# A decoder layer's query and key projections: one Newton operation moved to GpSimd, and a rotation that adds up in its PSUM bank

## The chip, the cores and the metric

The kernel runs on one core of one Trainium2 chip. The metric is the device time of one execution in microseconds (us); lower is better. The core has five engines with a queue of instructions each, worked through in order: TensorE (PE, matrix products), VectorE (DVE, elementwise), ScalarE (ACT, functions of one input), GpSimd (POOL, reductions across partitions and general work) and SyncE (SP, which only issues transfers here). Data lies in SBUF, and products land in PSUM, in eight banks.

## The reference

One decoder layer on 8 sequences of 100 tokens, width 1024, in float32: a retention block (8 heads), a cross-attention block with a context of 722 tokens (16 query heads, 4 key/value heads of 128), and a gated feed-forward block with 4096 hidden units, each followed by a residual sum and a layer norm. The change is in the second block's projections, of which the reference says:

```python
q = rms_norm(q, q_norm_w)          # x * rsqrt(mean(x*x, -1) + eps) * w, over a head's 128 numbers
k = rms_norm(k, k_norm_w)
...
q = q * cos + rotate_half(q) * sin
k = k * cos + rotate_half(k) * sin
k_full = jnp.concatenate([k_ctx, k], axis=1)
```

## The kernel before

Activations lie transposed: 128 features on the partitions, tokens along the row. The 800 tokens are worked on in two halves of N = 400. To keep float32 accuracy at the speed of the shorter format, each operand is split in a high and a low part, and each product is three matmuls (lines 91, 94 and 95): high by high, high by low, low by high. A projection of 1024 features to one head (`proj`) is 8 x 3 = 24 matmuls into one PSUM bank. The banks are shared out as three accumulators "a", four banks "s" and one "v".

The stages follow one another: the retention block, its output projection and norm, the second projections (the loop around lines 670 to 687), the attention over the context, its output projection and norm, the feed-forward block, and the last norm.

In the second projections a loop runs over 4 key/value heads, over pairs of weights (four for the first head), the two halves and the weights: four q heads, one k and one v per key/value head. So there are 40 groups of q or k and 8 of v; between them stand 4 halves of early context keys (`context_keys`, whose squares are summed on POOL too). For each q or k group:

- PE makes the projection in a bank "a".
- ACT squares it (L673), and POOL sums the squares over the partitions, to all of them (`all_red`, L141). `sq` and `ss` have two buffers each.
- `rope` rotates: ACT copies the two halves of the partitions, swapped, to a bank "s" (L149, L150); DVE multiplies the projection by the cosine to SBUF (L151), the swapped copy by the sine in its bank (L152), and adds them to SBUF (L153).
- `inv_root` makes the inverse root of sum + eps: ACT's logarithm with eps as bias (L128), exponential (L131) and square (L133) give a first guess r and its square, and one Newton step on DVE refines it: q = (sum + eps) * r*r (L134), then (q - 3) * r (L136). With `at=` a second bank "s" holds r and the result.
- DVE scales the rotated values (L678), ACT and DVE split them in high and low parts (L68, L69), and SP stores them to memory (L682), from where the attention loads them.

The order of each engine's instructions is not written out: the program is built with a scheduler that simulates the engines, and it reorders the work of the loop, within its dependences and its buffers. Some loads and norms are pinned. On POOL, the all-reduce and the elementwise operations belong to different libraries of code, and the build puts a library load ahead of an instruction whose library may not be resident. In this kernel there are two: one at the start, before an affine select that makes the identity matrix, and one before the first all-reduce.

Of the kernel before, what the change touches and what calls it, by code (L numbers as in the profile page):

```python
# [8 lines left out]
F32 = mybir.dt.float32  # L9
FR = mybir.dt.float32r  # L10
AF = mybir.ActivationFunctionType
ALU = mybir.AluOpType
# [4 lines left out]
P = 128  # L17
B, T, D = 8, 100, 1024
NB = 4
N = NB * T  # L20
# [20 lines left out]
def decoder_layer(ctx, tc, xT, cT, w1, wo1, w2, wo2, wc, w3, wd, gw, qw, kw, trig, dec, mask, out):  # L41
    nc = tc.nc

    def sbuf(name, bufs, side=None):
        return tc.tile_pool(name=name, bufs=bufs, side=side, reuse_waits="tile")
# [8 lines left out]
    def bank(tag):  # L54
        return ps.tile([P, 512], F32, tag=tag, name=tag, bufs=banks[tag])

    def f32(ap):
        return ap.bitcast(F32)

    def bt(ap):  # L60
        return ap.rearrange("p (b t) -> p b t", b=NB)
# [5 lines left out]
    def split2(hi, lo, src):  # L67
        nc.scalar.copy(hi, src)  # L68
        nc.vector.tensor_tensor(lo, src, f32(hi), ALU.subtract)  # L69

    def load_w(src, w=None, pinned=False):
        st = wp.tile([P, KT * P], F32, tag="wst", name="wst", bufs=3)
        if w is None:
            w = wp.tile([P, 2, KT * P], FR, tag="w", name="w", bufs=4)
        nc.sync.dma_start(out=st, in_=src)
        if pinned:
            tc.keep_in_program_order(nc.scalar.copy(w[:, 0], st))
            nc.vector.tensor_tensor(w[:, 1], st, f32(w[:, 0]), ALU.subtract)  # L78
        else:
            split(w, st)  # L80
        return w
# [6 lines left out]
    pin = tc.keep_in_program_order  # L88
# [25 lines left out]
    def proj(w, z, n=N, tag="a", todo=None):  # L114
        acc = bank(tag)[:, :n]
        for k in range(KT):
            pinned = between(todo, k)
            t = z[k // QT]
            mmw(acc, w, k, t[:, 0, k % QT, :n], t[:, 1, k % QT, :n], k == 0, k == KT - 1, pinned)
        return acc  # L120
# [1 line left out]
    def ln_exp():  # L122
        tc.keep_in_program_order(nc.scalar.preload_act_table_set(LN_EXP))

    def inv_root(pool, ss, eps, n=N, pin=False, at=None):

        r = pool.tile([P, n], F32, tag="r0", name="r0") if at is None else at
        ln = nc.scalar.activation(r, ss, AF.Ln, bias=eps)  # L128
        if pin:
            tc.keep_in_program_order(ln)  # L130
        nc.scalar.activation(r, r, AF.Exp, scale=-0.5)  # L131
        q = pool.tile([P, n], F32, tag="r1", name="r1")
        nc.scalar.activation(q, r, AF.Square)  # L133
        nc.vector.scalar_tensor_tensor(q, ss, eps, q, ALU.add, ALU.mult)  # L134
        out = q if at is None else at
        nc.vector.scalar_tensor_tensor(out, q, 3.0, r, ALU.subtract, ALU.mult)  # L136
        return out

    def all_red(pool, x, tag, op=RED.add):
        y = pool.tile([P, N], F32, tag=tag, name=tag)  # L140
        nc.gpsimd.partition_all_reduce(y, x, P, op)  # L141
        return y

    def rope(pool, acc, cosw, sinw, tag="t1", op=ALU.add, swapped=None):

        t1 = pool.tile([P, N], F32, tag=tag, name=tag)
        t2 = pool.tile([P, N], F32, tag="t2", name="t2") if swapped is None else swapped
        h = P // 2
        nc.scalar.copy(t2[0:h], acc[h:P])  # L149
        nc.scalar.copy(t2[h:P], acc[0:h])  # L150
        nc.vector.tensor_tensor(bt(t1), bt(acc), cosw[:, None, :].to_broadcast([P, NB, T]), ALU.mult)  # L151
        nc.vector.tensor_tensor(bt(t2), bt(t2), sinw[:, None, :].to_broadcast([P, NB, T]), ALU.mult)  # L152
        nc.vector.tensor_tensor(t1, t1, t2, op)  # L153
        return t1

    def tokens_first(pool, acc, copied=True):

        vt = acc
        if copied:
            vt = pool.tile([P, N], F32, tag="vt", name="vt", bufs=1)  # L160
            nc.scalar.copy(vt, acc)
        tr = bank("s")
        for b in range(NB):
            nc.tensor.transpose(tr[0:T, b * P:(b + 1) * P], vt[:, b * T:(b + 1) * T], ident)  # L164
        return tr[0:T]
# [30 lines left out]
    def const(v, name):  # L196
        t = cp.tile([P, 1], F32, name=name)
        nc.vector.memset(t, v)
        return t
# [3 lines left out]
    eps_k = const(128e-6, "eps_k")  # L203
# [238 lines left out]
    with sbuf("l1", 2) as p:  # L442
# [49 lines left out]
        qk, v, oo, ss = {}, {}, {}, {}  # L492
# [114 lines left out]
    def load_context(b):  # L607

        cz.clear()
        for hf in range(2):  # L610
            n = SN[hf]
            z = [big([P, 2, QT, SH]) for _ in range(2)]
            for k in range(0, KT, 2):
                cs = wp.tile([P, KT * P], F32, tag="wst", name="cs", bufs=3)
                cs = cs[:, :2 * n].rearrange("p (k n) -> p k n", k=2)
                nc.sync.dma_start(out=cs, in_=cT[b, :, k:k + 2, hf * SH:hf * SH + n])
                split(z[k // QT][:, :, k % QT:k % QT + 2, :n], cs)
            cz.append(z)

    def context_keys(kv):  # L620

        kall = ka.tile([P, 2, SC + T], FR, tag="kall", name="kall")
        wk = load_ws(2 * kv)
        sq = ka.tile([P, SC], F32, tag="ksq", name="ksq", bufs=1)
        ss = ka.tile([P, 6 * P], F32, tag="kss", name="kss", bufs=1)
        row = dr.tile([6, P], F32, tag="row", name="row", bufs=2)
        nc.gpsimd.memset(ss[:, SC:], 1.0)

        def step(hf):
            n, at = SN[hf], slice(hf * SH, hf * SH + SN[hf])  # L630
            acc = proj(wk, cz[hf], n)
            nc.scalar.activation(sq[:, at], acc, AF.Square)  # L632
            nc.gpsimd.partition_all_reduce(ss[:, at], sq[:, at], P, RED.add)  # L633
            nc.scalar.activation(kall[:, 0, at], acc, AF.Copy, scale=kws)
            nc.vector.scalar_tensor_tensor(kall[:, 1, at], acc, kws, f32(kall[:, 0, at]), ALU.mult, ALU.subtract)
            if hf:
                nc.sync.dma_start(out=row.rearrange("c p -> (c p)")[None, :], in_=ss[0:1])
        return step, (kall, row)
# [12 lines left out]
    with sbuf("l2", 2) as p:  # L651
        for kv in range(NKV):
            for i0, i1 in ((0, 4), (4, 6)) if kv == 0 else ((0, 2), (2, 4), (4, 6)):
                if (kv, i0) == (0, 4):
                    load_context(0)
                ws = [load_w(w2[kv, i]) for i in range(i0, i1)]
                if (kv, i0) in ((1, 2), (2, 2)):
                    step, kept = context_keys(kv - 1)
                    early.append(kept)
                if (kv, i0) in ((1, 2), (2, 0), (2, 2), (3, 0)):  # L660
                    step(i0 == 0)
                for half in range(2):
                    bs = slice(half * NB, (half + 1) * NB)
                    for i in range(i0, i1):
                        acc = proj(ws[i - i0], z1[half])
                        if i == 5:
                            tr = tokens_first(p, acc).rearrange("p (b d) -> p b d", b=NB)
                            vs = p.tile([T, NB, 2, P], FR, tag="vs", name="vs", bufs=1)
                            split2(vs[:, :, 0], vs[:, :, 1], tr)
                            nc.sync.dma_start(out=f32(vd[kv, :, bs]), in_=f32(vs))  # L670
                            continue
                        sq = p.tile([P, N], F32, tag="sq", name="sq")
                        nc.scalar.activation(sq, acc, AF.Square)  # L673
                        ss = all_red(p, sq, "ss")
                        tb = tq if i < 4 else tk
                        t = rope(p, acc, tb[:, 0], tb[:, 1], swapped=bank("s")[:, :N])
                        r = inv_root(p, ss, eps_k, at=bank("s")[:, :N])
                        nc.vector.scalar_tensor_tensor(  # L678
                            t, t, -0.5 if i < 4 else -0.5 * math.sqrt(P), r, ALU.mult, ALU.mult)
                        d = p.tile([P, NB, 2, T], FR, tag="d", name="d", bufs=3)  # L680
                        split2(d[:, :, 0], d[:, :, 1], bt(t))
                        nc.sync.dma_start(out=f32(qd[kv, i, :, bs] if i < 4 else kd[kv, :, bs]), in_=f32(d))  # L682
# [5 lines left out]
    with sbuf("cx", 2) as p, sbuf("c1", 1) as p1:  # L688
# [6 lines left out]
        for b in range(B):  # L695
            if b > 0:
                load_context(b)
            for kv in range(NKV):
# [10 lines left out]
                q = p.tile([P, 4, 2, T], FR, tag="q", name="q")  # L709
# [13 lines left out]
                r0 = p.tile([P, 6], F32, tag="rr0", name="rr0")  # L723
# [9 lines left out]
                s = p1.tile([P, NC, N], F32, tag="s", name="s")  # L733
# [5 lines left out]
                for j, c in enumerate(ORDER):  # L739
                    rows, n, t0 = (R6, N6, T6) if c == 6 else (P, N, 0)  # L740
# [35 lines left out]
                for j in (1, 0, 2, 3, 4, 5, 6):  # L776
                    c = ORDER[j]
                    n = N6 if c == 6 else N
# [4 lines left out]
                r = p.tile([P, N], F32, bufs=1, tag="r0", name="r0")  # L783
# [74 lines left out]
    for half in range(2):  # L858
        for i in range(2):
            ag, au = (proj(w, z2[half], tag=acc_tag()) for w in ws[i])  # L860
            t = temp()
# [221 lines left out]
    with sbuf("ln3", 1, "right") as lnp:  # L1083
        ws, todo = [], {}
        for half in range(2):
            y = rows(half)
            s1 = lnp.tile([P, N], F32, tag="s1", name="s1", bufs=2)
            for m in range(KT if half == 0 else KT - 2):
# [5 lines left out]
                acc = proj(ws[m], z3[half], tag=acc_tag(), todo=todo.pop(m, None))  # L1094
# [92 lines left out]
```

## Time and profile before

Median of three executions: 2505.04 us (2503.92 to 2506.51). The profiled execution took 2506.91 us, of which its span, the first to the last record, is 2505.1 us; the granted TensorE clock was 0.995 in the mean.

| | busy us | share of the span |
|---|---|---|
| TensorE (PE) | 2459.8 | 98% |
| VectorE (DVE) | 1952.1 | 78% |
| ScalarE (ACT) | 1340.7 | 54% |
| GpSimd (POOL) | 464.9 | 19% |
| the second projections, first to last square (L673) | | 612.0 to 836.1 us |

How to read the profile's lines: a group's line has the source line, engine, operation, output <- inputs, shapes and count, then busy time and the mean of one in ns, then the idle time of the engine just before these instructions and what ended it. A line of the timeline has the start and the duration in us, and in brackets the idle time before it and its releaser. "issue" is idle time in which the engine waited for nothing that the profile shows. A "q" behind an engine's name is its sequencer, which also issues transfers. In the stretches, each engine has its busy time and the number of instructions; PEclk is the clock that was granted to TensorE. Times of matmuls overlap, since they are pipelined.

### The profile page before, as it was taken

How to read it: one execution, taken by the hardware profiler on the slowest of the kernel's cores; microseconds unless marked ns; L12 is line 12 of the kernel's file. 1: busy time of each engine (PE TensorE's matmuls, PEld its weight loads, DVE VectorE, ACT ScalarE, POOL GpSimd, SP SyncE). 2: the span in 40 equal slices, each digit the busy share in tenths (PEclk: the TensorE clock that was granted, in tenths of full speed). 3: DMA queues.
4: the chain of work that ended last, by engine and by line, in shares of the span. 5: the costliest groups of instructions: out<-in, count | busy, mean ns of one | idle time of the engine just before them, and what ended most of it. 6: DMA issues, size and time to landing. Idle time of an engine off the chain costs nothing.

```text
span 2505.1 us, 37227 instructions
## 1 busy us (share of the span) xinstructions
PE 2459.8 (98%) x14068; PEld 2438.5 (97%) x14068; DVE 1952.1 (78%) x3101; ACT 1340.7 (54%) x2260; POOL 464.9 (19%) x234
## 2 busy tenths in 40 slices
PE   9999999997999999999999999999999999999997
PEld 9999999997899999999999999999999999999997
DVE  7678877567877688988989999866987777666756
ACT  6667676334767556566565666533544444432221
POOL 0111111001445343433434434100000000000000
PEclk9999999998999999999999999999999999999999
DMA  7333445774543654554554563675455444389731
GB/s 241 111 111 128 136 143 181 242 271 128 170 148 131 215 172 150 167 175 143 166 186 134 170 199 110 215 246 162 141 176 197 165 168 168 128 282 329 273 102 53
DMA packets 224451, 433.98 MB, mean 173 GB/s; under 512 B 47338, under 2 KB 168042, under 8 KB 211854
## 3 DMA queue, kind: packets, MB, share of 16 engines
q1 hardware_dynamic: 222542, 426.87, 50.7%
q0 software_dynamic: 1152, 4.19, 1.0%
q8 instruction: 111, 1.82, 0.3%
q14 instruction: 70, 0.57, 0.1%
q10 hardware_dynamic: 576, 0.52, 0.1%
HBM read 322.18 MB, written 109.35 MB: 172 GB/s over the span
## 4 chain that ended last, share of the span: by engine, by line
PE 91%; DVE 4%; DMA 3%; ACT 1%; issue 1%; POOL 0%; SPq 0%; DVEq 0%; ACTq 0%; POOLq 0%
PE a L95 19%; PE a L91 19%; PE a L94 19%; PE s L95 9%; PE s L94 9%; PE s L91 9%; PE v L95 1%; PE v L91 1%; PE v L94 1%; PE s L518 1%; PE s L716 1%; DMA cs<-in_cT 1%; DMA wst<-in_w 1%; PE s L164 1%; DVE big L69 0%
## 5 line engine op out<-in xcount | busy, mean ns | idle before, releaser
L91 PE MATMUL a<-big,w 128*128 128x400 f32 (+2 forms) x1808 | 609.0, 338 | 4.9 <-ACT big L68 1.8
L94 PE MATMUL a<-big,w 128*128 128x400 f32 (+2 forms) x1808 | 609.0, 337 | 0.7 <-DVE big L69 0.6
L95 PE MATMUL a<-big,w 128*128 128x400 f32 (+2 forms) x1808 | 608.1, 337 | 0.9 <-DVE w L78 0.9
L68 ACT CAST w<-wst 128x1024 fp32r<-128x1024 f32 (+1 forms) x229 | 237.5, 1039 | 389.5 <-PE s L95 134.6
L69 DVE TENSOR_TENSOR w<-wst,w 128x1024 fp32r<-128x1024 f32 (+1 forms) x229 | 280.5, 1226 | 137.8 <-ACT w L68 136.4
L91 PEld LDWEIGHTS a<-big,w 128*128 128x128 f32 x1808 | 339.6, 188 | 7.1 <-ACT big L68 2.3
L94 PEld LDWEIGHTS a<-big,w 128*128 128x128 f32 x1808 | 340.2, 188 | 2.5 <-DVE big L69 1.5
L95 PEld LDWEIGHTS a<-big,w 128*128 128x128 f32 x1808 | 340.2, 188 | 2.0 <-DVE w L78 1.3
L91 PE MATMUL a<-z,w 128*128 128x400 f32 x680 | 234.8, 345 | 21.2 <-DVE t L151 18.6
L95 PE MATMUL a<-z,w 128*128 128x400 f32 x680 | 235.8, 347 | 0.0
L94 PE MATMUL a<-z,w 128*128 128x400 f32 x680 | 235.7, 347 | 0.0
L91 PE MATMUL s<-big,w 128*128 128x400 f32 x664 | 230.5, 347 | 0.1
L95 PE MATMUL s<-big,w 128*128 128x400 f32 x664 | 229.0, 346 | 0.4 <-DVE w L69 0.4
L94 PE MATMUL s<-big,w 128*128 128x400 f32 x664 | 229.1, 345 | 0.0
L141 POOL PARTITION_ALL_REDUCE ss<-sq x56 | 150.9, 2697 | 328.2 <-DMA zd<-y 171.2
L633 POOL PARTITION_ALL_REDUCE kss<-ksq x64 | 167.2, 2613 | 130.3 <-ACT ksq L632 127.6
L91 PEld LDWEIGHTS a<-z,w 128*128 128x128 f32 x680 | 128.3, 189 | 23.0 <-DVE t L151 16.0
L750 ACT ACTIVATE s<-s,rk 128x400 f32<-128x400 f32 x160 | 87.8, 591 | 92.9 <-DVE sm L770 68.1
L95 PEld LDWEIGHTS a<-z,w 128*128 128x128 f32 x680 | 129.0, 190 | 0.3
L94 PEld LDWEIGHTS a<-z,w 128*128 128x128 f32 x680 | 128.2, 189 | 0.2
L91 PEld LDWEIGHTS s<-big,w 128*128 128x128 f32 x664 | 124.6, 188 | 1.4 <-ACT w L68 0.4
L95 PEld LDWEIGHTS s<-big,w 128*128 128x128 f32 x664 | 125.1, 188 | 0.7 <-DVE w L69 0.7
(361 smaller groups left out, 5439.3 us busy)
## 6 DMA issues: line engine op xcount, KB each, us to landing
wst<-in_w SPq DMA_DIRECT2D x135, 512.0 KB
w<-wcd SPq DMA_DIRECT2D x64, 1024.0 KB
wst<-in_wo SPq DMA_DIRECT2D x64, 512.0 KB
hd<-h SPq DMA_DIRECT2D x12, 1400.0 KB
wst<-in_wd SPq DMA_DIRECT2D x64, 256.0 KB
big<-o1d SPq DMA_DIRECT2D x16, 800.0 KB
qd<-d SPq DMA_DIRECT2D x32, 400.0 KB
q<-qd SPq DMA_DIRECT2D x32, 400.0 KB
```

Of the source, the lines that this page charges most:

```text
L68: nc.scalar.copy(hi, src)
L69: nc.vector.tensor_tensor(lo, src, f32(hi), ALU.subtract)
L91: i = nc.tensor.matmul(acc, lh, rh, start=start, stop=False, skip_group_check=chain)
L94: nc.tensor.matmul(acc, lh, rl, start=False, stop=False, skip_group_check=chain)
L95: nc.tensor.matmul(acc, ll, rh, start=False, stop=stop, skip_group_check=chain)
L141: nc.gpsimd.partition_all_reduce(y, x, P, op)
L164: nc.tensor.transpose(tr[0:T, b * P:(b + 1) * P], vt[:, b * T:(b + 1) * T], ident)
L518: nc.tensor.matmul(bt(o)[:, b], vv[:, b * P:(b + 1) * P], pf[:, b], start=True, stop=True)
L633: nc.gpsimd.partition_all_reduce(ss[:, at], sq[:, at], P, RED.add)
L716: nc.tensor.transpose(tr[0:rows, (c - c0) * P:(c - c0 + 1) * P], vt[:, c * P:c * P + rows], ident)
L750: nc.scalar.activation(sc, sp, AF.Copy, scale=rk[:, c:c + 1])
```

## The change

For the q and k groups of the second projections alone:

- The rotation's sum (L153 before) goes to the bank of the swapped copy in place of SBUF, and the scaling works on it there; the split reads the bank. `t1` is free after the sum.
- The first guess and its square lie in SBUF, so that one bank "s" serves a group in place of two.
- The first operation of the Newton step, (sum + eps) * r*r, leaves DVE. POOL adds eps to the sum in place, ACT's logarithm follows that addition and has no bias, and POOL multiplies by the square of the guess.
- The second operation, q - 3 times the guess, becomes q - 3 times the rotated values, and the scaling multiplies by the guess.

Other callers of `inv_root` and `rope` do what they did.

```diff
+    def root_guess(pool, ss, eps, n=N, pin=False):
+        r = pool.tile([P, n], F32, tag="r0", name="r0")
+        ln = nc.scalar.activation(r, ss, AF.Ln) if eps is None else nc.scalar.activation(r, ss, AF.Ln, bias=eps)
+        if pin:
+            tc.keep_in_program_order(ln)
         nc.scalar.activation(r, r, AF.Exp, scale=-0.5)
         q = pool.tile([P, n], F32, tag="r1", name="r1")
         nc.scalar.activation(q, r, AF.Square)
+        return r, q
+
+    def inv_root(pool, ss, eps, n=N, pin=False):
+        r, q = root_guess(pool, ss, eps, n, pin)
         nc.vector.scalar_tensor_tensor(q, ss, eps, q, ALU.add, ALU.mult)
-        out = q if at is None else at
-        nc.vector.scalar_tensor_tensor(out, q, 3.0, r, ALU.subtract, ALU.mult)
-        return out
+        nc.vector.scalar_tensor_tensor(q, q, 3.0, r, ALU.subtract, ALU.mult)
+        return q
...
-    def rope(pool, acc, cosw, sinw, tag="t1", op=ALU.add, swapped=None):
+    def rope(pool, acc, cosw, sinw, tag="t1", op=ALU.add, swapped=None, out=None):
...
-        nc.vector.tensor_tensor(t1, t1, t2, op)
+        nc.vector.tensor_tensor(t1 if out is None else out, t1, t2, op)
...
                         ss = all_red(p, sq, "ss")
                         tb = tq if i < 4 else tk
-                        t = rope(p, acc, tb[:, 0], tb[:, 1], swapped=bank("s")[:, :N])
-                        r = inv_root(p, ss, eps_k, at=bank("s")[:, :N])
+                        t = bank("s")[:, :N]
+                        rope(p, acc, tb[:, 0], tb[:, 1], swapped=t, out=t)
+
+                        nc.gpsimd.tensor_scalar_add(ss, ss, eps_k)
+                        r, q = root_guess(p, ss, None)
+                        nc.gpsimd.tensor_tensor(q, ss, q, ALU.mult)
+                        nc.vector.scalar_tensor_tensor(t, q, 3.0, t, ALU.subtract, ALU.mult)
                         nc.vector.scalar_tensor_tensor(
                             t, t, -0.5 if i < 4 else -0.5 * math.sqrt(P), r, ALU.mult, ALU.mult)
```

More of the change, by code (lines that the diff above doesn't have):

```diff
@@ L123, in ln_exp @@
         tc.keep_in_program_order(nc.scalar.preload_act_table_set(LN_EXP))
-    def inv_root(pool, ss, eps, n=N, pin=False, at=None):
-        r = pool.tile([P, n], F32, tag="r0", name="r0") if at is None else at
-        ln = nc.scalar.activation(r, ss, AF.Ln, bias=eps)
+    def root_guess(pool, ss, eps, n=N, pin=False):
+        r = pool.tile([P, n], F32, tag="r0", name="r0")
+        ln = nc.scalar.activation(r, ss, AF.Ln) if eps is None else nc.scalar.activation(r, ss, AF.Ln, bias=eps)
         if pin:
```

## The prediction

> **What bounds the kernel now.** I read the page's engine shares first, then the stretches of time around the edited loop, then GpSimd's (POOL's) own order of work, and last the groups of the edited lines.
>
> ```profile
> span 2505.1 us, 37227 instructions
> PE 2459.8 (98%) x14068; PEld 2438.5 (97%) x14068; DVE 1952.1 (78%) x3101; ACT 1340.7 (54%) x2260; POOL 464.9 (19%) x234
> PE 91%; DVE 4%; DMA 3%; ACT 1%; issue 1%; POOL 0%; SPq 0%; DVEq 0%; ACTq 0%; POOLq 0%
> ```
>
> TensorE (PE) is busy 98% of the span and is 91% of the chain that ended last. The edited loop runs from the first square (612.0 us) to the last (836.1). The stretches show busy time per engine and the granted clock:
>
> ```profile
> core 0: us, PE busy (x) PEld busy (x) DVE busy (x) ACT busy (x) POOL busy (x), PEclk, DMA share, GB/s
> 585.00:612.00 27.00, 15.33 (x80) 14.12 (x78) 23.14 (x39) 15.99 (x27) 0.00 (x0) 0.84 0.61 191
> 612.00:660.00 48.00, 39.56 (x204) 38.57 (x205) 42.63 (x74) 35.91 (x71) 27.69 (x10) 0.91 0.37 126
> 660.00:840.00 180.00, 178.71 (x999) 177.81 (x998) 137.32 (x240) 127.99 (x251) 90.40 (x38) 1.00 0.45 157
> ```
>
> From 660 on PE is full and VectorE (DVE) has a quarter of its time free. Only before 660 is PE short of work: 27.0 - 15.33 + 48.0 - 39.56 = 20.1 us. One group of the loop (24 matmuls, started about 0.182 us apart) costs PE 4.37 us; POOL needs 2.70 us of it, and idles the rest. These rows of POOL in order of time carry the forecast:
>
> ```profile
> 0.74 0.20 POOL masks.py:197 MEMSET ident<- 128x128 f32 x1 [0.29 <-POOLq L1175]
> 10.37 0.33 POOL masks.py:199 TENSOR_SCALAR_AFFINE_SELECT ident<-ident 128x128 f32<-128x128 f32 x1 [9.42 <-issue]
> 41.95 1.18 POOL L530 DMA_DIRECT2D wcd<-wst  x1 [31.26 <-DMA wcd<-w]
> 57.34 2.62 POOL L141 PARTITION_ALL_REDUCE ss<-sq  x1 [14.20 <-DVE sq L521]
> ...
> 612.59 7.88 POOL L141 PARTITION_ALL_REDUCE ss<-sq  x2 [171.20 <-DMA zd<-y]
> ...
> 836.67 2.60 POOL L141 PARTITION_ALL_REDUCE ss<-sq  x1 [6.14 <-PE s L164]
> 839.15 0.50 POOL L694 MEMSET ph<- 128x400 f32 x1
> ```
>
> The affine select stood idle 9.42 us before it started, and waited for nothing but a memset that ended at 0.94. What lay between is a change of POOL's code. The answer on that source line has it on POOL's sequencer:
>
> ```profile
> masks.py:199 POOLq MODIFY_POOL_CONFIG  x2: 11/11/11, 1.0 to 1.0; - x2
> ```
>
> The second and last such change stands at 43.1, ahead of the first all-reduce, and lies under the 14.20 us that this one waits for its data, which came 0.14 us before it started.
>
> **The change part by part.**
>
> *DVE loses the operation that is moved (L134).* The groups:
>
> ```profile
> L141 POOL PARTITION_ALL_REDUCE ss<-sq x56 | 150.9, 2697 | 328.2 <-DMA zd<-y 171.2 <-DVE sq L521 68.6 <-ACT sq L673 58.1
> L134 DVE SCALAR_TENSOR_TENSOR r<-ss,eps_k,r 128x400 f32<-128x400 f32 x40 | 25.1, 628 | 0.9 <-ACT r L133 0.9
> L136 DVE SCALAR_TENSOR_TENSOR s<-r,s 128x400 f32<-128x400 f32 x40 | 22.8, 571 | 0.2
> L153 DVE TENSOR_TENSOR t<-t,s 128x400 f32<-128x400 f32 x40 | 22.5, 564 | 0.2
> ```
>
> 40 x 0.628 = 25.1 us of DVE, worth nothing after 660, where DVE idles 42.7 of 180 us and PE does not wait; before it at most the 8.4 us that PE idles after 612. I take 0; the ends are -8.4 and 0.
>
> *Sum and scaling in the swapped copy's bank.* Writing to a bank or to SBUF makes little difference by L153 (0.564) and L136 (0.571), which do the one and the other. The logarithm and exponential, now to SBUF, and the split, now from a bank, stay near 0.5 us. Some hundredths of a microsecond on 40 groups, under PE: 0, within 4 us either way. Each group holds one score bank in place of two, but until its split; four banks are four groups of lookahead.
>
> *POOL gets an addition and a multiplication per group.* The trace has neither. From below the 400-wide POOL memset (0.50), which reads nothing; from above, for the addition, the affine select scaled by width, 0.331 x 400/128 = 1.03, and twice that, 2.06, for two operands. I take 0.75 and 1.20, about the middles, together 1.95 (ends 1.0 and 3.1).
>
> The Trainium skill (GPSIMD Engine Reference, section 3.1) gives 4497 ns for a two-input addition 2048 wide; by width that is an estimate of 0.88 us for the multiplication and 13 us less in the sum; no run here shows it.
>
> *POOL changes its code twice per group.* The built program of the changed kernel lists, between all-reduces and the new operations, 78 more library loads on POOL, alternating between library 0 (elementwise) and 1 (all-reduce); before has one of each. From the second round on POOL's order is: load 1, all-reduce of a group; load 0, multiplication of the group before, addition of this one. It is an in-order queue, so nothing passes a load. Its price R: 9.42 from the only row where nothing else was waited for; from above, 14.1, because the second was over when its data came; from below the nearest load of another engine's tables, ScalarE's (ACT's) 1.28. I take 9.42, as the row for the thing itself. It is a first load, at the start, beside busy DMA, so a cheaper one is possible.
>
> The Trainium skill (GPSIMD Engine Reference, section 2.1) puts the first call to freshly loaded code at about 6 us, 5.95 measured from the reconfiguration to the first instruction less an event wait. The row here has 9.42 with no wait seen; by the page's figure the sum would end near 2920 instead of 3187. It speaks against the change by either number.
>
> *The sum on POOL's queue,* from the first all-reduce at 612.6 to the last multiplication: 77 loads x 9.42 = 725.3 (the 78th follows it); 40 all-reduces x 2.70 = 107.9; 40 x 1.95 = 78.0; the four context-key all-reduces that stand in between, 4 x 2.43 = 9.7; and once, at the end, ACT's logarithm, exponential and square between addition and multiplication, 0.60 + 0.49 + 0.50 = 1.6. Together 922.5, so the last multiplication ends at 1535.1. A round is 2 x 9.42 + 2.70 + 1.95 = 23.5 us against PE's 4.37.
>
> *Who waits.* A square needs one of two buffers, free only after the all-reduce two groups earlier; the projections have three accumulators, which the squares and rotation release. So PE is never more than a few groups ahead, and goes at POOL's pace. No other PE work fills the gaps: in the built program its 40 q and k groups, 8 v groups and 4 context-key halves follow one another as before. ACT and DVE block at the logarithm and the second Newton operation, with rotations of the next groups behind them; the groups' lead of more than one round covers this. On SyncE's queue (SP) the stores of q and k come later, with weight loads queued behind them, but these stand some ten groups ahead of use. The number of SP rows is the same. PE's clock will fall in the gaps: after its one idle stretch of 15.6 us, up to 615.96, its rows show 13 matmuls 0.333 us apart instead of 0.182. A group then takes 24 x 0.182 + 13 x 0.15 = 6.3 us, still far below 23.5: 0.
>
> *The end.* Behind the last multiplication come two DVE operations and the split (0.57 + 0.56 + 0.53 + 0.57 = 2.2), which free the bank for the last transposes of the first context values: PE goes on at 1537.3. Before stood at that transpose at 853.3 (in TensorE's rows, four transposes of L716 that begin at 852.94 and take 0.60), but in the changed order 36 more matmuls (6.6 us) lie ahead of it; I credit half. What is left is 2505.1 - 853.3 - 3.3 = 1648.5, plus 2 for the clock: a span of 1537.3 + 1648.5 + 2 = 3188. The last load lies beside this PE work. The profiled execution took 2506.9, 1.8 over its span; the median, 2505.04, is 1.9 below that. So 3188 + 1.8 - 1.9 = 3188 stands for the time; I give 3187, from the unrounded terms.
>
> **The rivals.**
>
> *Loads in the middle of the kernel are cheaper.* For it: the row is a first load. At halfway between 1.28 and 9.42, 5.35 us, the sum loses 77 x 4.07 = 313: 2874.
>
> *They are dearer.* For it: nothing but the bound of 14.1: 77 x 4.7 = 362 more, 3549.
>
> *Not slower (the other side).* The libraries stay resident or the load runs under POOL's own waits, so R is next to nothing. Then a round is 2.70 + 1.95 = 4.65, all of it 40 x 4.65 + 9.7 + 1.6 = 197 us, inside the 240.7 that before has from 612.6 to 853.3; DVE's relief gives back up to 8.4, and the time is 2497 to 2505, with 2503 the likeliest. It decides where R is below (240.7 - 197)/77 = 0.57 us. Against it stands the 9.42 us row.
>
> *The new operations dear as well:* 3.1 instead of 1.95 adds 46, 3233; it only widens the forecast.
>
> **How the numbers follow.** Loads within 8 to 11.7 us (3187 likeliest): 0.60. Cheaper, 5.3 to 8: 0.23. Cheaper still, yet over 0.57: 0.05. Dearer: 0.08. Not slower: 0.04, half of it faster by over 0.2% (5 us, about what measuring this kernel can tell from no change). The range goes halfway to each bound of R, since the row is nearer than either: 5.35 (2874) to 11.75 (3187 + 77 x 2.33 = 3366), rounded to 2870 and 3370; the new operations' ends, -38 and +46, fit inside it around the likeliest. Slower: 0.96.
>
> **What would show it.** After: POOL has 80 pairs of reconfigurations, its elementwise rows stand idle about 9.4 us each "<-issue", squares come every 23 us or so, and PE's wait in that loop is put down to the rotation, squares or splits, with a share near 30% and the clock down in the gaps. DVE's L134 group for these tiles is gone, and what follows the loop looks as before, some 680 us later. The forecast is wrong if the idle time ahead of all-reduces is much shorter than 9.4, or if a round holds a wait besides POOL's own work: then the lookahead through ACT's and DVE's queues was too short.

## The result, and the profile after

The changed kernel takes 3009.56 us in the median of 4 executions (3007.24 to 3011.24), the kernel before 2504.99. The ratio is 1.2012, 95% interval 1.1998 to 1.2027: 20% slower. The profiled execution has a span of 3005.5 us, 500.4 more than before. The page's engine shares, and its slices of the span:

```profile
span 3005.5 us, 37487 instructions
PE 2550.8 (85%) x14068; PEld 2512.8 (84%) x14068; DVE 1941.9 (65%) x3061; ACT 1334.8 (44%) x2260; POOL 578.7 (19%) x314
PE   9999999945434443459999999999999999999998
PEclk9999999977767776779999999999999999999999
```

TensorE (PE) does the same 14068 matmuls, but in 8 of the 40 slices it is busy less than half of the time. They are the second projections. The busy times in that stretch, with the granted clock of TensorE in the third column from the right:

```profile
core 0: us, PE busy (x) PEld busy (x) DVE busy (x) ACT busy (x) POOL busy (x), PEclk, DMA share, GB/s
660.00:1300.00 640.00, 279.11 (x1175) 266.14 (x1175) 139.71 (x246) 144.44 (x287) 182.19 (x111) 0.71 0.16 55
```

No engine is busy for more than 44% of it, GpSimd (POOL) only for 28%. What fills POOL's time is told by its rows in order of time:

```profile
681.36 1.29 POOL L683 TENSOR_SCALAR ss<-ss,eps_k 128x400 f32<-128x400 f32 x1 [6.93 <-issue]
682.64 1.02 POOL L685 TENSOR_TENSOR r<-ss,r 128x400 f32<-128x400 f32 x1
689.52 2.62 POOL L145 PARTITION_ALL_REDUCE ss<-sq  x1 [5.85 <-issue]
698.89 1.02 POOL L685 TENSOR_TENSOR r<-ss,r 128x400 f32<-128x400 f32 x1 [6.75 <-issue]
699.91 1.29 POOL L683 TENSOR_SCALAR ss<-ss,eps_k 128x400 f32<-128x400 f32 x1
707.01 2.62 POOL L145 PARTITION_ALL_REDUCE ss<-sq  x1 [5.81 <-issue]
716.37 1.02 POOL L685 TENSOR_TENSOR r<-ss,r 128x400 f32<-128x400 f32 x1 [6.74 <-issue]
```

A round, from one all-reduce to the next, takes 17.5 us. 4.9 of it is work; twice POOL stands idle with nothing to wait for ("issue"), 5.8 us ahead of the all-reduce and 6.8 ahead of the elementwise pair. These are the changes of its code: the source line of the multiplication has them on POOL's sequencer.

```profile
L685 POOLq MODIFY_POOL_CONFIG  x64: 88/98/98, 639.2 to 1313.3; - x64
```

From the first reconfiguration record to the next POOL operation, the 78 loads take 502.3 us in all: 39 ahead of an all-reduce, 5.63 in the median, 222.4 in sum, and 39 ahead of an elementwise operation, 6.98 and 279.9. And the waits that follow from it, as groups:

```profile
L91 PE MATMUL a<-z,w 128*128 128x400 f32 x680 | 263.4, 387 | 326.0 <-DVE t L155 248.4
L686 DVE SCALAR_TENSOR_TENSOR s<-r,s 128x400 f32<-128x400 f32 x40 | 23.2, 579 | 485.5 <-POOL r L685 485.5
L145 POOL PARTITION_ALL_REDUCE ss<-sq x56 | 150.7, 2693 | 462.3 <-issue 223.8
L685 POOL TENSOR_TENSOR r<-ss,r 128x400 f32<-128x400 f32 x40 | 40.7, 1019 | 230.1 <-issue 229.6 <-POOL ss L683 0.6
```

VectorE (DVE) stands 485.5 us ahead of the second Newton operation, until POOL's product is there. Behind it in DVE's queue is a later group's rotation (L155), which frees the accumulator that PE waits for.

Where the 500.4 us are, by POOL's all-reduces (rounded):

| from, to | before us | after us | difference |
|---|---|---|---|
| start, first of the loop | 612.6 | 611.6 | -1.0 |
| first, last of the loop | 224.1 | 699.1 | +475.0 |
| last of the loop, first maximum of the attention | 28.2 | 33.8 | +5.6 |
| first maximum, last sum of the attention | 763.0 | 789.0 | +26.0 |
| the rest | 877.3 | 871.9 | -5.4 |

The loop is the loss. The attention, which no line of the change touches, has another 26 us.

### The profile page after: what moved, and what is told of

Same layout as the page of the kernel before. It is cut to its first block, busy times and chain, and to the rows that moved or that the text cites. A ratio compares the mean times of both kernels' runs of the same rounds, so it can differ in the third digit from the quotient of the medians.

```text
span 3005.5 us, 37487 instructions
## 1 busy us (share of the span) xinstructions
PE 2550.8 (85%) x14068; PEld 2512.8 (84%) x14068; DVE 1941.9 (65%) x3061; ACT 1334.8 (44%) x2260; POOL 578.7 (19%) x314
## 4 chain that ended last, share of the span: by engine, by line
PE 49%; DVE 3%; ACT 1%; DMA 1%; issue 1%; POOL 1%; SPq 0%; DVEq 0%; ACTq 0%
PE a L91 10%; PE a L95 10%; PE a L94 10%; PE s L95 5%; PE s L94 5%; PE s L91 5%; PE v L95 1%; PE v L91 1%; PE v L94 1%; DVE big L69 1%; DVE sm L779 0%; PE s L725 0%; DVE mx L760 0%; ACT s L759 0%; DMA w<-wcd 0%
## 5 line engine op out<-in xcount | busy, mean ns | idle before, releaser
L91 PE MATMUL a<-big,w 128*128 128x400 f32 (+2 forms) x1808 | 620.2, 344 | 87.5 <-DVE t L155 54.5
L95 PE MATMUL a<-big,w 128*128 128x400 f32 (+2 forms) x1808 | 615.6, 341 | 0.3 <-DVE w L78 0.3
L94 PE MATMUL a<-big,w 128*128 128x400 f32 (+2 forms) x1808 | 615.6, 342 | 0.2 <-DVE big L69 0.2
L91 PE MATMUL a<-z,w 128*128 128x400 f32 x680 | 263.4, 387 | 326.0 <-DVE t L155 248.4
L91 PEld LDWEIGHTS a<-z,w 128*128 128x128 f32 x680 | 146.5, 215 | 337.8 <-DVE t L155 256.8
L91 PEld LDWEIGHTS a<-big,w 128*128 128x128 f32 x1808 | 347.1, 192 | 93.6 <-DVE t L155 55.8
L94 PEld LDWEIGHTS a<-big,w 128*128 128x128 f32 x1808 | 348.0, 193 | 1.5 <-DVE big L69 1.2
L95 PEld LDWEIGHTS a<-big,w 128*128 128x128 f32 x1808 | 348.3, 193 | 1.2 <-DVE w L78 0.7
L686 DVE SCALAR_TENSOR_TENSOR s<-r,s 128x400 f32<-128x400 f32 x40 | 23.2, 579 | 485.5 <-POOL r L685 485.5
L94 PE MATMUL a<-z,w 128*128 128x400 f32 x680 | 258.3, 380 | 0.0
L95 PE MATMUL a<-z,w 128*128 128x400 f32 x680 | 256.2, 377 | 0.0
L637 POOL PARTITION_ALL_REDUCE kss<-ksq x64 | 187.6, 2931 | 352.8 <-ACT ksq L636 345.8
L94 PEld LDWEIGHTS a<-z,w 128*128 128x128 f32 x680 | 146.1, 215 | 0.5
L95 PEld LDWEIGHTS a<-z,w 128*128 128x128 f32 x680 | 145.8, 214 | 0.6
L91 PEld LDWEIGHTS s<-big,w 128*128 128x128 f32 x664 | 124.6, 188 | 1.4 <-ACT w L68 0.4
```

The lines of the kernel that those rows point to most:

```text
L91: i = nc.tensor.matmul(acc, lh, rh, start=start, stop=False, skip_group_check=chain)
L94: nc.tensor.matmul(acc, lh, rl, start=False, stop=False, skip_group_check=chain)
L95: nc.tensor.matmul(acc, ll, rh, start=False, stop=stop, skip_group_check=chain)
L686: nc.vector.scalar_tensor_tensor(t, q, 3.0, t, ALU.subtract, ALU.mult)
```

## The experiments

The theory, L: the library loads on POOL cost the time. The rivals: B, the sum and scaling in the swapped copy's bank; H, POOL's elementwise work and its hand-offs with ScalarE (ACT).

**The bank part alone.**

```diff
-                        nc.gpsimd.tensor_scalar_add(ss, ss, eps_k)
-                        r, q = root_guess(p, ss, None)
-                        nc.gpsimd.tensor_tensor(q, ss, q, ALU.mult)
+                        r, q = root_guess(p, ss, eps_k)
+                        nc.vector.scalar_tensor_tensor(q, ss, eps_k, q, ALU.add, ALU.mult)
```

> The bank part alone: the rotation's sum and the scaling stay in the swapped copy's bank, the first Newton operation is back on DVE, eps is the logarithm's bias again, and POOL does nothing but all-reduces. The built program has 2 library loads as before. Theory L (library loads on POOL cause the loss): 2495 to 2515 us, no rounds of 17 us in the loop. Rival B (one bank held until the split, or the reads and writes of PSUM, cause it): about 3000. Rival H (POOL's own elementwise work and the hand-offs POOL to ACT to POOL cause it): 2495 to 2515 too. Open besides: the context attention takes 26 us longer in the changed kernel; if that came from the scheduler's other order through the bank part, 2520 to 2535 here, if from the loads or the POOL part, nothing of it.

Measured: 2501.11 us against 2505.24, ratio 0.9984 (0.9975 to 0.9993): 4 us faster than before. B falls as a cause of the loss. The first to the last all-reduce of the loop takes 220.6 us against 224.1. One row that moved is the split's subtraction, of 26.6 us, mean 665 ns, before; it now reads the bank:

```profile
L69 DVE TENSOR_TENSOR d<-s,d 128x400 fp32r<-128x400 f32 x40 | 22.6, 565 | 4.3 <-ACT d L68 4.3
```

The attention takes 762.5 us here, so its 26 us do not come with the bank part.

**The POOL part alone.** Addition and multiplication on POOL, but the rotation adds to SBUF and a second bank holds the guess.

```diff
-                        t = bank("s")[:, :N]
-                        rope(p, acc, tb[:, 0], tb[:, 1], swapped=t, out=t)
...
+                        t = rope(p, acc, tb[:, 0], tb[:, 1], swapped=bank("s")[:, :N])
...
-                        r, q = root_guess(p, ss, None)
+                        r = bank("s")[:, :N]
...
-                        nc.vector.scalar_tensor_tensor(t, q, 3.0, t, ALU.subtract, ALU.mult)
+                        nc.vector.scalar_tensor_tensor(r, q, 3.0, r, ALU.subtract, ALU.mult)
```

> The POOL part alone: addition and multiplication on POOL as in the changed kernel, but the rotation adds to SBUF, and a second bank holds the guess, as before the change. The built program has 82 loads more than before (78 in the changed kernel). Theory L: the loss stays and grows with the loads, 3010 + 4 x 6.4, about 3035 us (2990 to 3080). Rival B (the bank part): 2505 to 2540.

Measured: 3015.63 us in one execution. The whole loss is in the POOL part. The loop takes 731.9 us with its 82 loads, and the attention 754.4, which is less than before: loads in the loop do not by themselves slow the attention.

**Loads with next to no work.**

```diff
...
+                        e = p.tile([P, 2], F32, tag="e", name="e")
+                        nc.gpsimd.tensor_scalar(e[:, 0:1], ss[:, 0:1], 0.0, eps_k, ALU.mult, ALU.add)
+                        r, q = root_guess(p, ss, e[:, 0:1])
+                        nc.gpsimd.tensor_scalar(e[:, 1:2], q[:, 0:1], 0.0, 3.0, ALU.mult, ALU.add)
+                        nc.vector.scalar_tensor_tensor(q, ss, e[:, 0:1], q, ALU.add, ALU.mult)
+                        nc.vector.scalar_tensor_tensor(t, q, e[:, 1:2], t, ALU.subtract, ALU.mult)
```

> Loads with next to no work: the first Newton operation is on DVE at full width, and POOL's two operations per group are shrunk to one column, in the same places of the chain (they make the eps that the logarithm and DVE use, and the 3.0 of the second operation). The built program has 66 loads more than before, where the changed kernel has 78. Theory L: 66 x 6.4 + 40 x 2.7 + some 25 is a loop of about 560 us instead of 714, so about 2855 us (2800 to 2920). Rival H (the work's length): POOL's work falls to nearly nothing, so 2505 to 2560.

Measured: 2886.19 us, one execution. The groups of POOL's two operations in this run:

```profile
L684 POOL TENSOR_SCALAR e<-ss,eps_k 128x1 f32<-128x1 f32 x40 | 10.1, 255 | 125.9 <-issue 125.9
L686 POOL TENSOR_SCALAR e<-r 128x1 f32<-128x1 f32 x40 | 9.4, 237 | 156.7 <-issue 115.6 <-ACT r L133 41.1
```

Their work has fallen from 92.3 us (51.6 + 40.7) to 19.5, the idle time ahead of them has stayed, and three quarters of the loss with it. From the first all-reduce to the end of the last of these operations, as L counted, it is 613.1 us, 53 over what L said; the 66 loads take 438.3, 6.64 each.

**Work without loads.** POOL copies are built without a library load.

```diff
...
+                        nc.gpsimd.tensor_copy(ss, ss)
+                        r, q = root_guess(p, ss, eps_k)
+                        nc.gpsimd.tensor_copy(q, q)
+                        nc.vector.scalar_tensor_tensor(q, ss, eps_k, q, ALU.add, ALU.mult)
```

> Work without loads: in the two places of the chain POOL copies the 128x400 sum and the 128x400 square onto themselves, which the build issues without a library load (2 loads in all, as before); the arithmetic is on DVE. Theory L: 2500 to 2535 us (a round is 2.7 plus two copies of 0.5 to 1.3 us, at or little above PE's 4.4). Rival H (work and hand-offs on POOL): about 2900 to 3000.

Measured: 2552.72 us, ratio 1.0185 (1.0171 to 1.0199). Over 90% of the loss is gone, so H is not its main cause; but 47 us remain, more than L allowed.

**The hand-offs alone,** to find these 47 us: the same copies, one column wide.

```diff
-                        nc.gpsimd.tensor_copy(ss, ss)
+                        nc.gpsimd.tensor_copy(ss[:, 0:1], ss[:, 0:1])
...
-                        nc.gpsimd.tensor_copy(q, q)
+                        nc.gpsimd.tensor_copy(q[:, 0:1], q[:, 0:1])
```

> As the run with POOL copies and no loads (2552.7 us), but the copies are one column wide, so that the hand-offs POOL to ACT to POOL remain and nearly no work on POOL; 2 loads as before. If the 47 us of that run came from the hand-offs (POOL's in-order queue waits for ACT's square ahead of the next all-reduce): 2535 to 2555. If from the width of the copies: 2500 to 2515.

Measured: 2506.34 us, ratio 1.0000 (0.9990 to 1.0009). In this run's order of the queue the hand-offs cost nothing. The full-width copies cost only 0.60 and 0.56 us each, 45.5 in all; with an all-reduce that is some 3.8 us a group, less than PE's 4.37. What differs as well is the order of POOL's queue, which the scheduler chose anew. At full width it often put two groups' second copies one after the other, ahead of the next all-reduces, where they wait for ACT's square:

```profile
681.48 0.52 POOL L685 COPY r<-r 128x400 f32<-128x400 f32 x1 [4.66 <-ACT r L133]
683.56 1.14 POOL L685 COPY r<-r 128x400 f32<-128x400 f32 x1 [1.55 <-ACT r L133]
685.22 2.60 POOL L145 PARTITION_ALL_REDUCE ss<-sq  x1 [0.52 <-DVE r L686]
```

Over the loop this wait comes to 85.1 us; with one column it is 26.8. Whether the order or the width makes the 47 us was not separated.

**The two real operations, nearly without loads.** The sum over partitions goes to PE.

```diff
-                        ss = all_red(p, sq, "ss")
+                        sm = bank("v")[:, :N]
+                        nc.tensor.matmul(sm, onem, sq, start=True, stop=True)
+                        ss = p.tile([P, N], F32, tag="ss", name="ss")
+                        nc.scalar.activation(ss, sm, AF.Copy, scale=float(D))
```

> The changed kernel's two POOL operations stay as they are, at full width, but the sum of squares over the partitions goes from POOL to PE (a matmul with the matrix of 1/1024, in bank v, copied out by ACT times 1024). POOL then changes its code only around the four context-key all-reduces: 10 loads more than before. Theory L (loads): the loop loses most of its loss; 10 loads of 6.4, partly beside other work, and 40 matmuls of about 0.8 give 2530 to 2620 us. Rival H (the elementwise work on POOL and its hand-offs to ACT): 1.3 + 1.0 us of work and both hand-offs are still there, 2850 to 3010.

Measured: 2556.07 us, ratio 1.0196 (1.0180 to 1.0211). POOL's addition (1.45 us in the mean) and multiplication (1.09) are all there, at full width, and 90% of the loss is gone. What remains lies ahead of the attention: for the 40 new matmuls PE has 80 more records of 0.498 us, and ahead of them it waits 60.0 us in all for ACT's squares.

**Fewer loads, the same arithmetic:** two q groups share one round on POOL.

```diff
-                        ss = all_red(p, sq, "ss")
+                        ii = [i, i + 1] if i < 4 else [i]
+                        m = len(ii)
...
+                        nc.gpsimd.partition_all_reduce(ss[:, 0:m], sq[:, 0:m], P, RED.add)
+                        nc.gpsimd.tensor_scalar_add(ss[:, 0:m], ss[:, 0:m], eps_k)
...
+                        nc.gpsimd.tensor_tensor(q[:, 0:m], ss[:, 0:m], q[:, 0:m], ALU.mult)
```

> Fewer loads, the same arithmetic: two q groups share one all-reduce, one addition and one multiplication on POOL, 800 wide; k groups stay single. 24 rounds in place of 40, 52 loads more than before (78 in the changed kernel). Theory L: loads 52 x 6.44 = 335, all-reduces 16 x 5.2 + 8 x 2.7 = 105, elementwise work 40 x 2.31 = 92, some 10 more: a loop of about 545 us in place of 699, 2830 to 2900. A rival by which each group costs its 17.5 us whatever the loads (the chain of waits): 3010.

Measured: 2843.09 us, one execution, within what L said; the loop is 530.9 us for 545, and the attention takes 793.1, of which L had said nothing.

**The product alone on POOL.**

```diff
-                        nc.gpsimd.tensor_scalar_add(ss, ss, eps_k)
-                        r, q = root_guess(p, ss, None)
+                        r, q = root_guess(p, ss, eps_k)
                         nc.gpsimd.tensor_tensor(q, ss, q, ALU.mult)
```

> Only the multiplication on POOL; the addition is gone (eps is the logarithm's bias, and is left out of the product, so the operation computes sum x r x r in place of (sum + eps) x r x r). 72 loads more than before. Theory L: the loads stay, and the loop is shorter by 6 x 6.4 and at most 40 x 1.3: 2910 to 2985 us. If the two elementwise operations' work were what counts: less than half of the loss left, below 2750.

Measured: 2905.06 us, one execution, 5 below L's range. Taking away one of the two operations leaves four fifths of the loss, because the loads stay. The attention is back at 762.3 us, which is part of the difference.

Together, the loops, from the first to the last all-reduce, against the loads that lie in them (each from its first reconfiguration record to the next POOL operation; the last two loads of a run stand behind its last all-reduce):

| | loads in it | loop us | loads us | loop less loads |
|---|---|---|---|---|
| bank part alone | 0 | 220.6 | 0 | 220.6 |
| pairs | 50 | 530.9 | 329.9 | 201.0 |
| loads with tiny work | 64 | 600.3 | 421.7 | 178.6 |
| product alone | 70 | 622.6 | 452.6 | 170.0 |
| changed kernel | 76 | 699.1 | 488.6 | 210.5 |
| POOL part alone | 80 | 731.9 | 520.0 | 211.9 |

The price of a load is 6.4 to 6.6 us in all five, whatever the work, and what is left beside the loads is less than the loop takes without any.

**The 26 us in the attention.** POOL's rows show two orders of its queue there. In the changed kernel and in the run with pairs, three of four all-reduces of a unit's sums stand behind one context-key all-reduce more than in the kernel before and in most runs: the tenth, for example, has 25 of them ahead of it in the changed kernel and 24 before. In the changed kernel's rows the context-key all-reduce (L637) waits for its square, and the sums (mb<-sm) come behind it:

```profile
1705.43 2.75 POOL L637 PARTITION_ALL_REDUCE kss<-ksq  x1 [9.34 <-ACT ksq L636]
1708.46 2.60 POOL L145 PARTITION_ALL_REDUCE mb<-sm  x1 [0.28 <-DVE sm L779]
1715.75 2.38 POOL L637 PARTITION_ALL_REDUCE kss<-ksq  x1 [4.68 <-ACT ksq L636]
```

The sums in these rows lost nothing by it: their last addition on DVE ended 0.09 us before they started. Two kernels that differ from the changed one in the loop's last groups alone tell order from loads. One:

```diff
+                        if kv == 3 and i >= 4:
+                            r, q = root_guess(p, ss, eps_k)
+                            nc.vector.scalar_tensor_tensor(q, ss, eps_k, q, ALU.add, ALU.mult)
+                        else:
...
```

> The changed kernel, but the last two groups (the k groups of the last key/value head) have the first Newton operation on DVE. 76 loads more than before, where the changed kernel has 78. In the built program, POOL's queue in the attention keeps the changed kernel's order, in which each all-reduce of a unit's sums stands behind a context-key all-reduce of a later unit. If that order costs the 26 us that the attention takes longer: from the first maximum's all-reduce to the last sum's some 789 us, as in the changed kernel. The whole: 3010 minus one to two rounds of 17.5, 2970 to 3005.

and the other with `i >= 2`:

> The same with the last six groups (the second and third q pair's last two q and the k of the last head, both halves) on DVE: 68 loads more than before. In the built program, POOL's queue in the attention is then in the order of the kernel before. If the order costs the 26 us: 763 us from the first maximum's all-reduce to the last sum's; if the loads or the late start of the stage cost it: about 789 again. The whole: the other run minus some 4 rounds of 17.5, and minus 20 to 26 if the order is the cause, 2870 to 2930.

Measured: 3007.77 us with 789.1 in the attention, and 2929.09 with 756.9, one execution each. The waits of POOL in the attention, of the first and of the second:

```profile
POOL kss L637 <- ACT ksq L636: 339.5, 51, 13.9
```

```profile
POOL kss L637 <- ACT ksq L636: 94.6, 35, 5.7
```

With 68 loads ahead of it and a start some 430 us later than before, the second has an attention as fast as before's, and its queue is in the old order. By this stage's time every run falls on its queue's side: 789.0, 793.1 and 789.1 with the one order, 754 to 763 with the other. So neither the loads nor the late start cost the 26 us; they go with the order that the scheduler chose. How that order costs them is open: TensorE idles 17.6 us of this stage in the changed kernel, 14.0 of them put down to VectorE's split of the context keys (L639), and 0.5 in the kernel before. No run changed POOL's order alone, so the orders of other engines may have their share. The first run's whole was expected up to 3005 and came out 3 us above.

## Why the prediction was right and where it was off

*Direction and mechanism: right.* POOL became the bound of the loop by its code loads, PE follows at its pace, and the clock falls in the gaps (0.71). That cost nothing that the loop shows: with PE's rows 0.33 us apart, as at 702.16, 702.50 and 702.83 us, a group's 24 matmuls take 8 us of a round's 17.5. Squares come every 17.5 us where 23.5 was forecast.

*"Its price R": mis-sized.* This term carries the error. 9.42 was taken from the first load of the program. In the loop, a load takes 5.63 us ahead of an all-reduce and 6.98 ahead of an elementwise operation, 6.44 in the mean: 77 x (9.42 - 6.44) = 229 us less. The same first load at the program's start takes 8.76 in the changed kernel and 8.8 to 9.8 in the other profiles, dearer each time than the loop's mean; why, no run shows:

```profile
9.70 0.49 POOL masks.py:199 TENSOR_SCALAR_AFFINE_SELECT ident<-ident 128x128 f32<-128x128 f32 x1 [8.76 <-issue]
```

The two bounds held, but the choice of the nearest row was wrong: the first use was not like the seventieth. The case "cheaper, 5.3 to 8", given a chance of 0.23 and priced by 5.35 at 2874, is what happened, and not the case of 0.60. The Trainium skill's 5.95 us (GPSIMD Engine Reference, section 2.1), which would have made 2920, lay nearer than the row: it falls between the two prices measured.

*"POOL gets an addition and a multiplication": a little too low.* 1.29 + 1.02 = 2.31 where 1.95 was taken, 14 us more. The addition, with one full-width input and a column of eps, costs more than the upper bound from the affine select, 1.03, and more than the multiplication with two. The Trainium skill's two-input rate (GPSIMD Engine Reference, section 3.1), by width an estimate of 0.88, is a little under the 1.02 measured.

*The queue's sum.* 922.5 was forecast; from 611.6 to the end of the last multiplication at 1325.7 it is 714.1. 922.5 - 229 + 14 = 707 leaves 7 us for which the forecast had no term.

*"Who waits": right.* The lookahead covered ACT's and DVE's waits; POOL's rows in the loop stand idle 504.0 us under "issue", nearly all of it behind reconfigurations, and 0.6 for another operation.

*"The end": 27 us short.* From the last multiplication to the end 1652.7 were forecast, 1679.8 measured. The forecast took what follows the loop as unchanged; the attention took 26 us longer, with the scheduler's other order. That order of POOL's queue could be read in the built program beforehand. With the loads (229 less), the two operations (14 more) and the 7 us, this makes up the 182 us, within 1, by which the profiled span, 3005.5, fell short of the 3188 forecast.

*The bank part and DVE's relief: 0 within 4 us, and 0 to 8.4.* The bank part alone gains 4 us, at the edge of its bounds. What DVE's 25 us of relief bought cannot be told beside the loads.

*The other-side rival,* loads that cost next to nothing, needed R below 0.57; no load took less than 5.4.

## What to carry to other kernels

Before work goes to an engine because it idles, ask what the engine must do to change over: here 2.3 us of work per group brought 12.6 us of code loads, since the all-reduce and the elementwise operations need different libraries. Copies, memsets and all-reduces lived together without loads; grouping the operations of one library, as the pairs did, divides the price. A first use at a program's start is a poor measure of the steady price, and where a scheduler orders queues, a change in one stage can reorder the next: compare the built orders of the stages behind it as well. The version to keep is the bank part alone, 0.16% faster than before.

## What the runs showed of the hardware

A load of POOL's library leaves only records of 1 to 98 ns on its sequencer in the loop, and 5.4 us or more up to the next operation, put down to "issue" as idle time. "Issue" alone is no sign of a load: in the run with the sum on PE, POOL's multiplications stand idle 98.7 us under it, most of them with no reconfiguration ahead. As two libraries alternate, each load is paid again in full, also in a stretch with little DMA traffic (share 0.16). The price depends on what comes next: 5.6 to 5.8 us before an all-reduce and 7.0 to 7.2 before an elementwise operation in the medians of the runs with 52 loads or more. An operation one column wide took 0.24 to 0.26 us on POOL where the same kind at 400 columns took 1.29.
